# A cross-attention kernel on one core: the scaled gamma and beta made on ScalarE, x's two halves normalised one after the other, and a new table of the order of all calls

## The chip, the cores and the metric

The kernel runs on one core of a Trainium2 chip. The metric is the device time of one execution in microseconds (us), lower is better; a kernel's time is the median of several executions. A core has five engines, each with a queue of its own that it works through in order: TensorE (PE, matmuls; its weight loads are listed as PEld), VectorE (DVE), ScalarE (ACT), GpSimd (POOL) and SyncE (SP, which here only starts DMA transfers). They meet only at semaphores: an instruction at the head of its queue waits until what it reads has been written and what it overwrites has been read. The transfers themselves run on 16 DMA engines that all queues share.

## The reference, cut

```python
# x, ctx: (8, 256, 1024) float32; mask: (8, 256), all true; 32 heads of 32
mu  = mean(x, -1);  var = mean((x - mu)**2, -1)
xn  = (x - mu) * rsqrt(var + 1e-5) * gamma + beta
Q   = split_heads(xn @ Wq.T)                  # (8, 32, 256, 32)
K = V = split_heads(ctx)
scores = einsum('bhsd,bhtd->bhst', Q, K) / sqrt(32)
probs  = softmax(where(mask, scores, -inf), -1)
attn   = einsum('bhst,bhtd->bhsd', probs, V)
out = x + merge_heads(attn) @ Wout.T
```

All matrix products are in float32.

## The kernel before, in words

**Recording and order.** After a few set-up instructions (among them `make_identity`, which writes the 128x128 unit matrix `ident` into the tile `ring` on POOL), the kernel replaces `nc` by `Recorded(nc)` (L356). From there on nothing is issued: each call is only appended to a list, as engine, operation and arguments, and its number is its place in that list, 0 to 6577. The last line of the kernel (L1721) is `nc.issue(ORDER, OTHER)`, which issues the recorded calls in the order of the table `ORDER`, a long string of numbers and ranges (`OTHER` could give a call to another engine and is empty). All calls are issued at one line of that helper, so nearly every row of the profile says L374; the tile names tell them apart. As every engine works through its own queue, only the order of two calls of one engine matters to the time. There is a schedule by hand, so nothing reorders the calls afterwards.

**Work.** Batch b and a group g of four heads make a slot n = 8b+g, 64 in all. In each slot:

- PE makes the scores of the four heads (tile `sc`, eight matmuls of `k` with the projected query `qa`),
- DVE adds the mask and takes the row's extreme (`e`, `mn`), ACT takes the exponential with its row sum (`e<-e,mn`), POOL or ACT scales by the reciprocal sum (`rden`),
- DVE transposes `e` in 32x32 blocks into `pT`; ACT copies half of `pT` aside into `pc`; four DMAs on SP's queue then swap rows between partitions: `pT<-pT` twice, and later `pT<-pc` twice,
- PE forms probabilities times values (`pv`), in many small matmuls from `pT` and `v_all`. `v_all` is one buffer for two slots' values; its next load, on SP's queue, waits until the slots before have read it.

Between these, PE projects the next batch's query (`pq`, and `pq_P` for most batches) from the transposed, normalised input `xnT` and the weights `wq`, and multiplies the results with the output weights `wo` (`po`). Both products are done for pairs of batches in a scheme of seven products instead of eight, which needs sums of blocks of `wq` and `wo` (made on POOL and DVE, some of them kept in device memory by stores on SP's queue: calls 1356 and 1636 are two of those, of half a block sum each). From batch 2 on, `xnT` is also put in place by DMAs on SP (`xnT<-xe`).

**The head.** The change's two lines and most of the prediction stand here. The calls, with their numbers in the list:

- 0 to 31: 32 transposes of `ident` into a tile `busy` that nobody reads. They keep PE running while there is nothing else to do; the table strews them.
- 32, 33: loads of gamma (`gam`) and beta (`bet`), 128x8 each, on ACT's queue. 34 to 37: x of batch 0 (`x`) in four quarters, on SP's queue, as are all of the following: 38, 41 and 43 to 45, 50 to 52 and others, the blocks of `wq` (512 KB each), `k`, the mask and x of the next batches (`load_*`, L466 to L540; issued L558 to L580).
- 55, 56 (L1427, L1428): `gs` = s·gamma and `bs` = s·beta with s = -1/sqrt(32), each 128x8; `bs` is the same tile as `bet`, scaled in place. Before, both are TENSOR_SCALARs on POOL.
- 57 to 60, then 63 to 66 (`ln_stats`, L587): for each half of x_0 (128 of its 256 rows), two BATCH_NORM_STATS on DVE (`st`), their combination (`mv`) and the addition of the epsilon (`ve`); 61 and 67: the power -0.5 on POOL (`rstd`).
- 62 and 86 (`ln_norm`, L612): DVE normalises a half of x in place, 128x1024.
- 68 to 75 (`transpose_x0`, L632): PE transposes the first half's eight 128x128 blocks into `px`; 97 to 104 the second's.
- 76 to 83 (`copy_x0`, L641): the eight blocks go to `xnT` with the scale `gs` and shift `bs`: five on ACT (76, 77, 78, 80, 83: ACTIVATE Identity), three on DVE (79, 81, 82). These are the first ACTIVATEs of the kernel, and ACT's table of functions is loaded ahead of the first of them.
- 84, 85: POOL copies of `bs` into an extra column of `xnT` and of a sum (`h_s1`); both read `bs`.
- 87 to 94 (`first_q`, L650): PE projects the first query block, eight matmuls into `pq`; 95 copies it to `qa`. 105 to 108: scores of slot 0's first half, from `k` and `qa`; then the stream of `pq` matmuls for the second half and the next blocks.

## Time and profile before

| what | value |
|---|---|
| median of 3 runs | 567.06 us (566.14, 570.87, 567.06) |
| the profiled execution's own time | 569.71 us |
| span of the profiled execution | 567.9 us |
| granted TensorE clock over the span | 0.997 |
| instructions | 18645 |
| bytes moved by DMA, mean rate | 113.67 MB, 200 GB/s |

The page gives each engine's busy time and share of the span; then the span in 40 slices of 14.2 us, one digit for the busy tenths of each slice; then the chain of work that ended last, followed back from the last instruction. A row of the timeline reads: start, busy length, engine, line, operation, output<-inputs, partitions x elements and type, how many instructions the row joins, and in square brackets how long the engine had stood idle before it and what released it. In the list of waits, a row names the waiting engine and tile, the work that released it, then total idle time, count and the longest. In the table of stretches, a row has the stretch and its length, then the busy time of PE, PEld, DVE, ACT and POOL with instruction counts, the granted clock, the DMA engines' mean busy share and the GB/s moved. The last rows of the kind "wq<-in_wq_dram SPq ..., 512.0 KB, 9.9" give the median us from the issue of a DMA to its landing. `ring` in a row is the tile that holds the unit matrix at first and sums of blocks later.

### The profile page before, as it was taken

To read this page: it belongs to the slowest core of one execution; us is meant where nothing else is said; L and a number is where in the kernel's file an instruction comes from. 1 tells how busy PE (TensorE), PEld (TensorE's weight loads), DVE (VectorE), ACT (ScalarE), POOL (GpSimd) and SP (SyncE) were. 2 spreads that over 40 slices of the span, in tenths; PEclk is the share of its full clock that TensorE was granted. 3 is DMA by queue.
4 is the path that set the end of the run, shared out by engine and by line. 5 is a ranking of instruction groups with operands and counts; after the bars stand their busy time and mean duration, and the time that the engine had idled before them with its cause. 6 is when DMAs were issued, how large, how long until landed. Compare 5 with 4: busy or idle time off the path is not lost.

```text
span 567.9 us, 18645 instructions
## 1 busy us (share of the span) xinstructions
PE 556.1 (98%) x6570; PEld 371.1 (65%) x6570; DVE 464.3 (82%) x1703; ACT 436.4 (77%) x1461; POOL 410.4 (72%) x621
## 2 busy tenths in 40 slices
PE   6999999998999999999999999999999999999997
PEld 6777776666666766667766676666676577655544
DVE  5899999786988799888878999978767988887724
ACT  2698889785886679878777779879858678979930
POOL 2688989995988976468877955368855777375681
PEclk9999999998999999999999999999999999999999
DMA  8898667687677889797566776778856765674533
GB/s 302 333 268 233 184 173 188 191 238 184 212 222 190 248 216 215 207 265 225 139 191 202 219 203 187 185 215 227 230 136 199 198 169 153 184 220 99 151 94 112
DMA packets 48325, 113.67 MB, mean 200 GB/s; under 512 B 9960, under 2 KB 11624, under 8 KB 48232
## 3 DMA queue, kind: packets, MB, share of 16 engines
q1 hardware_dynamic: 42232, 92.55, 58.4%
q0 software_dynamic: 5712, 19.93, 11.5%
q8 instruction: 52, 0.85, 0.7%
q14 instruction: 41, 0.34, 0.2%
q10 hardware_dynamic: 288, 0.01, 0.0%
HBM read 59.91 MB, written 12.70 MB: 128 GB/s over the span
## 4 chain that ended last, share of the span: by engine, by line
PE 77%; DMA 7%; DVE 7%; ACT 4%; issue 2%; SPq 1%; POOL 1%; DVEq 0%; ACTq 0%
PE pq_P L374 23%; PE po_S L374 17%; PE pv L374 10%; PE sc L374 10%; PE po_A L374 10%; DMA pT<-pT 4%; PE po_end L374 3%; DVE e L374 3%; DVE pT L374 2%; ACT e L374 2%; PE pq L374 2%; DMA pT<-pc 2%; PE ph_P L374 1%; PE po_last L374 1%; SPq L374 1%
## 5 line engine op out<-in xcount | busy, mean ns | idle before, releaser
L374 ACT ACTIVATE e<-e,mn 128x256 f32<-128x256 f32 x512 | 256.1, 502 | 57.8 <-DVE mn L374 45.5
L374 POOL TENSOR_SCALAR e<-e,rden 128x256 f32<-128x256 f32 x368 | 172.2, 480 | 120.6 <-DVE rden L374 118.5
L374 DVE STREAM_TRANSPOSE pT<-e 128x512 f32<-128x512 f32 x256 | 176.7, 700 | 35.9 <-POOL e L374 26.4
L374 DVE CUSTOM_DVE_ANT_0 e<-sc,mb 128x256 f32<-128x256 f32 x512 | 192.6, 410 | 6.0 <-PE sc L374 2.8
L374 PE MATMUL pq_P<-xnT,wq 128*128 128x256 f32 x544 | 132.4, 383 | 0.2 <-DVE qa L374 0.2
L374 PEld LDWEIGHTS pq_P<-xnT,wq 128*128 128x128 f32 x544 | 102.1, 190 | 45.0 <-issue 29.7
L374 ACT ACTIVATION_READ_ACCUMULATOR e<-e,mn 128x1 f32 x512 | 97.0, 190 | 0.0
L374 ACT COPY pc<-pT 128x512 f32<-128x512 f32 x128 | 75.7, 611 | 11.1 <-DMA pT<-pc 6.4
L374 PE MATMUL po_S<-wo,at 128*128 128x512 f32 x152 | 74.5, 601 | 0.0
L374 PE MATMUL pv<-pT,v_all 64*32 64x128 f32 x3584 | 61.5, 277 | 3.0 <-issue 2.1
L374 PEld LDWEIGHTS pv<-pT,v_all 64*32 64x32 f32 x3584 | 53.0, 107 | 14.6 <-issue 9.0
L374 PE MATMUL po_A<-wo,at 128*128 128x512 f32 x128 | 60.9, 602 | 0.0
L374 DVE RECIPROCAL rden<-den 128x2 f32<-128x2 f32 x228 | 32.7, 152 | 29.1 <-ACT e L374 27.8
L374 PE MATMUL po_S<-wo,s 128*128 128x512 f32 x104 | 51.1, 602 | 0.1
L374 PE MATMUL sc<-k,qa 32*128 32x256 f32 x640 | 48.6, 402 | 0.6 <-DMA k<-in_kv_dram 0.5
L374 ACT ACTIVATE e<-e,rden 128x256 f32<-128x256 f32 x88 | 41.5, 502 | 7.0 <-DVE rden L374 6.5
L374 ACT COPY at<-pv 128x128 f32<-128x128 f32 x128 | 30.1, 253 | 17.5 <-PE pv L374 17.5
L374 PEld LDWEIGHTS sc<-k,qa 32*128 32x128 f32 x640 | 30.4, 184 | 19.1 <-issue 8.3
L374 DVE DVE_READ_ACCUMULATOR2_ANT mn<- 128x1 f32 x512 | 42.6, 83 | 0.0
L374 PEld LDWEIGHTS po_S<-wo,at 128*128 128x128 f32 x152 | 27.9, 190 | 19.4 <-issue 15.6
L374 PEld LDWEIGHTS po_A<-wo,at 128*128 128x128 f32 x128 | 23.3, 190 | 22.5 <-issue 19.6
L374 PE MATMUL pq<-xnT,wq 128*128 128x256 f32 (+3 forms) x144 | 31.7, 363 | 1.1 <-ACT xnT L374 0.8
(121 smaller groups left out, 685.8 us busy)
## 6 DMA issues: line engine op xcount, KB each, us to landing
pT<-pT SPq DMA_DIRECT2D x128, 128.0 KB, 3.8
pT<-pc SPq DMA_DIRECT2D x128, 128.0 KB, 4.0
v_all<-in_kv_dram POOLq DMA_DIRECT2D x17, 512.0 KB, 5.7
k<-in_kv_dram SPq DMA_DIRECT2D x30, 256.0 KB, 3.8
r<-in_x_dram SPq DMA_DIRECT2D x26, 256.0 KB, 4.6
xnT<-xe SPq DMA_DIRECT2D x92, 64.0 KB, 3.9
out_dram<-r POOLq DMA_DIRECT2D x18, 256.0 KB, 4.1
wq<-in_wq_dram SPq DMA_DIRECT2D x8, 512.0 KB, 9.9
```

What stands on the lines that cost most here:

```text
L374: getattr(getattr(self.nc, other.get(i, engine)), name)(*a, **k)
```

## The change

The two lines that make `gs` and `bs` become ACTIVATEs with the function Copy on ACT:

```diff
-    nc.gpsimd.tensor_scalar(gs, gam, NEG_SCALE, 1.0, ALU.mult, ALU.mult)
-    nc.gpsimd.tensor_scalar(bs, bs, NEG_SCALE, 1.0, ALU.mult, ALU.mult)
+    nc.scalar.activation(gs, gam, AF.Copy, scale=NEG_SCALE)
+    nc.scalar.activation(bs, bs, AF.Copy, scale=NEG_SCALE)
```

And the whole table `ORDER` is another one. The calls are the same 6578 but for these two; their order is new throughout. Its first rows, and those with the calls that the prediction speaks of (1348 is the load of `v_all` for slots 10 and 11; 1212 and 1213 the `pT<-pc` pair of slot 11; 1356 and 1636 the stores of block sums):

```diff
-32-33 35 34 36-38 43 40 39 42 41 44 51 50 46 45 54-55 0-19 56 58 57 59-60 64 84-85 61-63 65-71 20-24 72-74
-25-26 76-78 80 86-87 75 27 79 82-83 81 88-89 28 97-98 29 90-91 99 92 30 93-95 100-102 31 103-109 111-112 110
-132 123-126 171 170 172 96 114 173 116 119 113 117 115 127-128 133-134 129-131 135 120 137 136 138 121 145-146
...
-1391-1392 1389-1390 1403 1220 1402 1395 1394 1405 1332 1407-1408 1406 1399 1415 1414 1435 1361 1636 1356 1145
-1137-1138 1143 1210 1217 1139 1208 1008 1141 1146 1206 1140 1209 1218 1207 1144 1348 1212 1010 1213 1011
...
+32-33 35 34 36-38 42 40 43 39 41 50 44 47 52 45-46 54 56 55 58 57 59-60 85 0-15 61-62 64 63 65-66 68 16 69-70
+17 71 18-20 72 21-22 73-77 23-25 80-81 78 83-84 67 86-87 26 79 82 88 27-28 89 29-30 97-98 90-95 101 99 31 102
+100 103-112 132 123-126 133 170 96 113 115-117 114 127-130 145-146 171 119-120 131 134 121-122 118 135-136
...
+1009 1139 1008 1214 1212-1213 1010 1148 1219 1314 1348 1362-1369 1373-1378 1297-1298 1379 1299 1380 1300 1387
...
+1435 1573-1580 1445-1508 1513-1516 1429 1555 1354 1581 1636 1422 1356 1421 1631 1353 1641 1544-1546 1434 1520
```

Read by engine, the new head is this. ACT: 56 then 55, then the copies 76, 77, 80, 78, 83. POOL: 85, then 61 (the first `rstd`), then 84 and 67. DVE: the first half's statistics, 62 (its norm), then 64, 63, 65, 66 (the second half's statistics), 81, then 86 (its norm), then 79 and 82; before, 64 stood ahead of 62, and 86 ahead of all three copies. PE: 16 of the `busy` transposes ahead of the first transpose of x (20 before), the others strewn between the next calls. SP: x_0, `wq` block 0, block 1, the mask, x_1's second half, `k`, x_1's first half, then `wq` blocks 5, 2, `k`, 7, 3, 4, x_2, block 6; before: x_0, `wq` block 0, x_1's second half, the mask, `k`, block 1, x_1's first half, blocks 2, 6, 5, 4, 3, x_2, block 7, `k`. Counted per engine, 576 of PE's 3317 calls stand at another place among PE's calls than before, 999 of DVE's 1191, 799 of ACT's 950, 519 of POOL's 612 and 422 of SP's 506. In SP's queue the load of `v_all` 1348 is 139th (136th before), and the stores 1636 and 1356 are 149th and 151st (117th and 118th before).

## The prediction

> **What bounds the kernel now.** I read the page first: the engines' shares, the 40 slices, the chain that ended last.

> ```profile
> span 567.9 us, 18645 instructions
> ...
> PE 556.1 (98%) x6570; PEld 371.1 (65%) x6570; DVE 464.3 (82%) x1703; ACT 436.4 (77%) x1461; POOL 410.4 (72%) x621
> ...
> PE   6999999998999999999999999999999999999997
> ...
> PE 77%; DMA 7%; DVE 7%; ACT 4%; issue 2%; SPq 1%; POOL 1%; DVEq 0%; ACTq 0%
> ```

> TensorE (PE) has matmuls in flight for 556.1 of 567.9 us; all but the first slice is nearly full. The change removes no matmul. So it can gain only where PE waits: at the head, and in a few holes. The list of waits, for PE in the first 20 us, names the head's:

> ```profile
> PE px L374 <- DVE x L374: 1.9, 1, 1.9
> PE busy L374 <- POOL ring masks.py:199: 1.8, 1, 1.8
> PE pq L374 <- ACT xnT L374: 0.8, 1, 0.8
> ```

> The timeline shows this head (start, length, engine, operation; in brackets the idle time before it and what ended it):

> ```profile
> 1.76 4.45 PE L374 MATMUL busy<-ring 128*128 128x128 f32 x20 [1.76 <-POOL ring masks.py:199]
> ...
> 4.43 0.21 POOL L374 TENSOR_SCALAR bet<-bet 128x8 f32<-128x8 f32 x1 [0.52 <-DMA bet<-in_beta_dram]
> ...
> 4.84 0.19 POOL L374 COPY ring<-bet 128x4 f32<-128x4 f32 x1
> ...
> 5.42 0.57 POOL L374 TENSOR_TENSOR rstd<-ve,mhalf 128x1 f32<-128x1 f32 x1 [0.39 <-DVE ve L374]
> ...
> 6.60 0.69 DVE L374 BATCH_NORM_STATS2 st<-x 128x6 f32<-128x512 f32 x1 [1.27 <-DMA x<-in_x_dram]
> 7.21 0.80 DVE L374 TENSOR_SCALAR x<-x,mv,rstd 128x1024 f32<-128x1024 f32 x1
> 7.92 0.69 DVE L374 BATCH_NORM_STATS2 st<-x 128x6 f32<-128x512 f32 x1
> 8.06 0.66 PE L374 MATMUL px<-ring,x 128*128 128x128 f32 x4 [1.86 <-DVE x L374]
> ...
> 8.55 0.71 PE L374 MATMUL busy<-ring 128*128 128x128 f32 x5
> ...
> 8.80 1.28 ACT L374 ACT_TABLE_LOAD   x1 [8.80 <-PE px L374]
> ...
> 9.70 0.81 DVE L374 TENSOR_SCALAR x<-x,mv,rstd 128x1024 f32<-128x1024 f32 x1 [0.67 <-POOL rstd L374]
> 10.10 1.50 ACT L374 ACTIVATE xnT<-px,bet,gs 128x128 f32<-128x128 f32 x4
> ...
> 10.61 0.49 PE L374 MATMUL pq<-xnT,wq 128*128 128x128 f32 x2 [0.80 <-ACT xnT L374]
> ...
> 11.25 0.73 DVE L374 TENSOR_SCALAR xnT<-px,gs,bet 128x128 f32<-128x128 f32 x2 [0.73 <-PE px L374]
> ...
> 12.56 0.41 DVE L374 TENSOR_SCALAR xnT<-px,gs,bet 128x128 f32<-128x128 f32 x1 [0.59 <-ACT xnT L374]
> ...
> 14.66 0.71 PE L374 MATMUL sc<-k,qa 32*128 32x256 f32 x8
> ...
> 15.30 3.79 PE L374 MATMUL pq<-xnT,wq 128*128 128x257 f32 x24
> ```

> Two things here are later than they must be. VectorE (DVE) could normalise the first half of x when rstd ends at 5.42+0.57 = 5.99, but stands before a statistic whose x lands at 6.60, so it starts at 7.21. And ScalarE (ACT) loads its table only when the transposes end at 8.80, 1.28 us on the path. From 15.30 on PE streams.

> **The change, step by step.** POOL loses two tile operations of 0.2 us; ACT gains two ACTIVATEs over 128x8. No row shows that shape. Between the 0.19 us of a 128x4 copy and the 0.27 us of a 128x128 copy I take 0.20, as 8 columns are nearest to 4; the ends differ by 0.14 us over the two. The table load goes ahead of them. In the row above it began when the wait of its ACTIVATE ended, so I let it wait here for beta, which the new table puts first: 4.43. If it does not wait, it is hidden altogether; that end saves another 0.7 us (below).

> First half: load 4.43 to 5.71, bs to 5.91. POOL's queue now has the copy of bs (call 85) **ahead** of the first rstd (call 61): copy 5.95 to 6.14, rstd 6.14 to 6.71. That is 0.72 later than 5.99: a new wait, and behind it stands only what needs rstd. Normalising then runs 6.75 to 7.55 instead of 7.21 to 8.01, and the transposes start at 7.60, 0.46 earlier. The new table puts two filler transposes between the first four, 0.11 each; ACT started 0.74 after them, now 0.74+0.22, at 8.56, and has its table. So the first xnT starts at 8.58 instead of 10.10: **1.52 earlier** (0.46+1.28-0.22).

> Second half: both statistics now follow the norm on DVE, 1.35 us from 7.55 to 8.90. Statistics to norm took 9.70-8.61 = 1.09 before, so the norm runs 9.99 to 10.80, 0.29 **later** than before (9.70 to 10.51). It stays off the path: the last three DVE copies of the first half ended at 12.56+0.41 = 12.97. In the new order one goes before this norm and two (0.73) after it, to 11.55, so 1.42 earlier. The scores stood 1.69 behind that last copy; now 13.24, and the stream starts at 13.88 instead of 15.30. Gain at the head: **1.4 us**.

> Do the loads keep up? Rows by stretch (busy times, then clock, DMA share, GB/s):

> ```profile
> 0.00:3.00 3.00, 1.24 (x6) 1.25 (x7) 0.00 (x0) 0.00 (x0) 1.11 (x8) 1.00 0.29 96
> 3.00:6.00 3.00, 3.00 (x16) 2.88 (x14) 1.75 (x4) 0.00 (x0) 1.30 (x5) 1.00 1.03 337
> 6.00:9.00 3.00, 1.14 (x11) 0.94 (x10) 2.33 (x5) 0.20 (x1) 0.00 (x0) 1.00 0.94 320
> 9.00:12.00 3.00, 2.20 (x20) 1.96 (x19) 1.58 (x4) 2.59 (x5) 0.55 (x1) 1.00 0.97 367
> ```

> By 6.0 us 1.30 MB have moved, by 9.0 2.26, by 12.0 3.36. The four x blocks (1.05 MB) are through at 5.3 and were seen at 6.60, so 1.3 us of notice. wq's first block (1.57 MB) comes at 6.9+1.3 = 8.2, before its first use at 8.58+0.51 = 9.09. k, now behind wq's second block (2.95 MB), comes at 10.9+1.3 = 12.2, 1.0 ahead of the scores. x_1's second half (2.7 MB) comes at 10.2+1.3 = 11.5, when DVE reaches its statistic at 11.55. Of the wq blocks, 2, 4 and 6 stand further back than before; block 6 by most, behind a load that waits for x's buffer:

> ```profile
> 14.76 0.33 SPq L374 DMA_DIRECT2D x<-in_x_dram  x1
> ...
> 25.88 1.28 POOL L374 TENSOR_TENSOR wo<-wq 128x512 f32<-128x512 f32 x1
> ...
> wq<-in_wq_dram SPq DMA_DIRECT2D x8, 512.0 KB, 9.9
> ```

> Issued at 15.09-1.4 = 13.7 it lands by the median of 9.9 at 23.6; POOL's sums read it second now, at 25.88-1.4+1.28 = 25.8. Each of these covers is 0 to 2 us thick; where one is gone, its reader waits as long as the load is late.

> The rest of the table swaps neighbours. Scores stay in runs of eight, values in runs of 32 and 64 head matmuls; what alternates more finely is projection with output products, which costs nothing where operands are there. The holes are where it could matter. The worst, from the chain, the timeline, the DMA view and the stretches:

> ```profile
> 129.65 2.08 issue
> ...
> 122.95 0.53 SPq L374 DMA_DIRECT2D v_all<-in_kv_dram  x1
> ...
> 124.47 0.61 SPq L374 DMA_DIRECT2D xnT<-xe  x1
> ...
> 125.17 0.54 SPq L374 DMA_DIRECT2D pT<-pc  x1
> ...
> v_all<-in_kv_dram SPq DMA_DIRECT2D x1, 512.0 KB, 8.7
> ...
> 132.00:134.00 2.00, 2.00 (x98) 2.00 (x97) 0.41 (x1) 1.58 (x5) 1.81 (x3) 0.57 0.55 150
> 134.00:136.00 2.00, 2.00 (x48) 1.50 (x33) 1.97 (x7) 1.47 (x6) 1.64 (x2) 0.58 0.30 68
> ```

> PE stands from 129.65 to 131.73 for v_all, issued at 122.95 and landed 8.7 us later; then the clock runs at 0.57, which loses 2 x 0.43 + 2 x 0.42 = 1.7 us more. In the new table this load is three places further back in SP's queue (139th, was 136th), 3 x 0.6 = 1.8 us, but two stores of wq halves (1 MB) now stand behind it and not ahead, so it may land faster. Bounds for this place: the hole gone, -3.8; v_all held until the second pT<-pc has gone, +4.7 (below). I take 0, as both effects are of one size.

> Sum: 569.7 us (the profiled execution's own time; 567.9 is its span) less 1.4 is 568.3. That run lies 2.65 above the median of the three runs, 567.06, so against the median 565.66; I say **565.6**, own range 563.5 to 568.

> **Rivals.** (1) *More comes free:* the load waits for nothing (rstd back at 5.42, another 0.7 earlier) or the hole at 129.65 closes. For it: 1 MB of stores no longer stands ahead of v_all. Against it: v_all's own place is later. With the hole gone: 567.06-1.4-3.8 = 561.9.
> (2) *Slower: v_all waits behind a swap.* SP issues in order; the new table has the second pT<-pc of the same pair ahead of v_all, and three xnT moves. If that pT<-pc goes no earlier than 125.17, v_all goes at 125.17+0.54+3 x 0.61 = 127.6, 4.6 later, lands at 136.3, and PE stands 6.7 instead of 2.1 us: 567.06-1.4+4.6 = 570.3. It decides once v_all is issued over 1.4 us later relative to PE.
> (3) *PE starts cold.* The first twenty transposes took 4.45 us, 0.22 each; from 8.06 on a spacing of 0.11. The new table has sixteen before the wait, 3.5 us. If that no longer brings the fast rate, six transposes before ACT's start cost 0.66 more, and eight pq steps up to 1.8: 566.3 to 568.1, say 567.0. [...]

> (4) *ACT is not ready behind its load.* If another 1.28 us stands there (a second table, or something after the load), bs, the first rstd and the norm come that much later, and the gain at the head is 0.1 to 0.2: 566.9. Against it: the load ends at 10.08 and the next ACTIVATE starts at 10.10, and that one load (x1 in the row, and no other in the view by lines) served Identity, Copy and Exp alike. [...]

> **How the numbers follow.** Forecast 0.50, rival (1) 0.18, (2) 0.13, (3) 0.14, (4) 0.05. A step of 1% is 5.7 us, about what a measurement of this kernel tells from no change. Over 1% faster (below 561.4) is about half of rival (1) and a little of unseen holes: 0.12. Over 1% slower (above 572.7) needs a second hole beside rival (2): 0.04. The rest, 0.84, is within 1%. The range takes in most of (1) and (2) whole: 560.5 to 571.

> **What would show it.** Right: ACT's table load starts near 4.4 and ends before the transposes; rstd ends near 6.7; norm near 6.8; first xnT near 8.6; PE's long pq stream starts near 13.9 with wq never its releaser; the hole before pv near 128 is about 2 us. Wrong: a table load at 0 or a second one; PE waiting for wq or k before 25 us; transposes at 0.22 after 7.6; a head gain that is there at 14 and gone by 140, then a hole took it. If the median is below 561 or above 571, not the head but the rest of the table decided, and the step that costed it at 0 failed.

## The result and the profile after

The changed kernel takes 564.01 us (median of 19 runs, 560.58 to 568.27) against 566.87 us before (19 runs, 563.64 to 571.93): ratio 0.9936, 95% interval 0.991 to 0.9962. (A ratio is given here as it was recorded with its interval; it is not the quotient of the two medians, which would be 0.995.) It is faster by about 0.6%, inside the 1% that the prediction took as the bound. The forecast was 565.6, its own range 563.5 to 568. The profiled execution took 564.37 us, against 569.71 before.

The page after, in the lines that the prediction began with (span, engines, the chain that ended last):

```profile
span 562.6 us, 18616 instructions
...
PE 553.0 (98%) x6570; PEld 368.9 (66%) x6570; DVE 467.3 (83%) x1703; ACT 436.3 (78%) x1463; POOL 410.2 (73%) x619
...
PE 90%; DVE 6%; DMA 2%; issue 1%; POOL 1%; ACT 1%; SPq 0%; DVEq 0%; ACTq 0%; POOLq 0%
```

The work is the same; the chain now runs through PE for 90% of the span (77% before), as fewer steps of it hang on transfers (DMA 2%, 7% before). The list of PE's waits, here in part, has at its top one that was not there before, for a sum of blocks of `wo`:

```profile
PE po_S L374 <- POOL wo L374: 1.9, 1, 1.9
...
PE px L374 <- DVE x L374: 1.6, 1, 1.6
PE ph_P L374 <- DVE qa L374: 0.6, 1, 0.6
```

The head, from the timeline (columns as in the prediction):

```profile
1.64 1.28 ACT L374 ACT_TABLE_LOAD   x1 [1.64 <-PEq L1750]
...
4.46 0.21 ACT L374 ACTIVATE bet<-bet 128x8 f32<-128x8 f32 x1 [1.54 <-DMA bet<-in_beta_dram]
...
4.73 0.19 POOL L374 COPY ring<-bet 128x4 f32<-128x4 f32 x1 [3.03 <-ACT bet L374]
...
5.56 0.56 POOL L374 TENSOR_TENSOR rstd<-ve,mhalf 128x1 f32<-128x1 f32 x1 [0.64 <-DVE ve L374]
...
6.15 0.81 DVE L374 TENSOR_SCALAR x<-x,mv,rstd 128x1024 f32<-128x1024 f32 x1 [0.75 <-POOL rstd L374]
...
7.30 0.38 PE L374 MATMUL px<-ring,x 128*128 128x128 f32 x2
...
8.00 1.90 ACT L374 ACTIVATE xnT<-px,bet,gs 128x128 f32<-128x128 f32 x5 [3.23 <-PE px L374]
...
9.33 0.80 DVE L374 TENSOR_SCALAR x<-x,mv,rstd 128x1024 f32<-128x1024 f32 x1
...
10.05 0.72 DVE L374 TENSOR_SCALAR xnT<-px,gs,bet 128x128 f32<-128x128 f32 x2
...
13.23 3.79 PE L374 MATMUL pq<-xnT,wq 128*128 128x257 f32 x24
```

The load of ACT's table waited for nothing; it was over at 2.92. The first xnT copy starts at 8.00 (10.10 before), the long pq stream at 13.23 (15.30 before): 2.07 us earlier.

Where the two profiled executions part can be followed by matching each matmul with the same call's matmul in the profile of before. PE's lead (median over 20 us each) is 2.1 at 20 us, 1.5 at 80, 5.2 at 120, 2.7 at 140, 3.4 at 200, 4.0 at 400 and 5.35 at the end. The lead grows at 130 because before stood still for v_all there (2.08 us), and shrinks at 134 because the changed kernel stands still for a wo sum (1.88 us). Two things had to be explained: whether the head's 2.07 us are there in every execution, and where the new wait comes from.

### The profile page after: what moved, and what is told of

Its sections match the earlier page's. It is cut to its first block, busy times and chain, and to the rows that moved or that the text cites. A ratio compares the mean times of both kernels' runs of the same rounds, so it can differ in the third digit from the quotient of the medians.

```text
span 562.6 us, 18616 instructions
## 1 busy us (share of the span) xinstructions
PE 553.0 (98%) x6570; PEld 368.9 (66%) x6570; DVE 467.3 (83%) x1703; ACT 436.3 (78%) x1463; POOL 410.2 (73%) x619
## 3 DMA queue, kind: packets, MB, share of 16 engines
q0 software_dynamic: 5712, 19.93, 11.5%
## 4 chain that ended last, share of the span: by engine, by line
PE 90%; DVE 6%; DMA 2%; issue 1%; POOL 1%; ACT 1%; SPq 0%; DVEq 0%; ACTq 0%; POOLq 0%
PE pq_P L374 26%; PE po_S L374 19%; PE sc L374 11%; PE pv L374 11%; PE po_A L374 10%; PE pq L374 4%; PE ph_P L374 3%; PE po_end L374 3%; DVE pT L374 2%; DVE e L374 1%; DMA v_all<-in_kv_dram 1%; PE po_last L374 1%; DVE ring L374 1%; PE px L374 1%; DMA x<-in_x_dram 1%
## 5 line engine op out<-in xcount | busy, mean ns | idle before, releaser
L374 ACT ACTIVATE e<-e,mn 128x256 f32<-128x256 f32 x512 | 256.4, 503 | 60.2 <-DVE mn L374 53.1
L374 POOL TENSOR_SCALAR e<-e,rden 128x256 f32<-128x256 f32 x368 | 172.4, 483 | 105.4 <-DVE rden L374 89.9
L374 DVE STREAM_TRANSPOSE pT<-e 128x512 f32<-128x512 f32 x256 | 175.6, 699 | 31.5 <-POOL e L374 20.2
L374 DVE CUSTOM_DVE_ANT_0 e<-sc,mb 128x256 f32<-128x256 f32 x512 | 191.3, 410 | 6.0 <-PE sc L374 3.8
L374 PE MATMUL pq_P<-xnT,wq 128*128 128x256 f32 x544 | 133.2, 382 | 0.0
L374 PEld LDWEIGHTS pq_P<-xnT,wq 128*128 128x128 f32 x544 | 101.9, 190 | 46.9 <-issue 31.5
L374 ACT ACTIVATION_READ_ACCUMULATOR e<-e,mn 128x1 f32 x512 | 97.4, 190 | 0.0
L374 ACT COPY pc<-pT 128x512 f32<-128x512 f32 x128 | 76.7, 612 | 8.3 <-DVE pT L374 6.0
L374 PE MATMUL po_S<-wo,at 128*128 128x512 f32 x152 | 75.3, 600 | 1.9 <-POOL wo L374 1.9
L374 PE MATMUL po_A<-wo,at 128*128 128x512 f32 x128 | 61.1, 601 | 0.0
L374 PE MATMUL pv<-pT,v_all 64*32 64x128 f32 x3584 | 59.1, 272 | 0.3 <-DMA v_all<-in_kv_dram 0.3
L374 PEld LDWEIGHTS pv<-pT,v_all 64*32 64x32 f32 x3584 | 51.3, 105 | 11.3 <-issue 6.4
L374 DVE RECIPROCAL rden<-den 128x2 f32<-128x2 f32 x228 | 33.1, 152 | 27.8 <-ACT e L374 27.2
L374 PE MATMUL po_S<-wo,s 128*128 128x512 f32 x104 | 51.2, 602 | 0.0
L374 ACT ACTIVATE e<-e,rden 128x256 f32<-128x256 f32 x88 | 41.4, 502 | 11.6 <-DVE rden L374 10.8
L374 PE MATMUL sc<-k,qa 32*128 32x256 f32 x640 | 47.9, 401 | 0.0
L374 DVE DVE_READ_ACCUMULATOR2_ANT mn<- 128x1 f32 x512 | 42.3, 83 | 0.0
L374 ACT COPY at<-pv 128x128 f32<-128x128 f32 x128 | 29.8, 256 | 15.4 <-PE pv L374 15.4
L374 PEld LDWEIGHTS sc<-k,qa 32*128 32x128 f32 x640 | 30.0, 184 | 17.6 <-issue 7.2
L374 PEld LDWEIGHTS po_S<-wo,at 128*128 128x128 f32 x152 | 28.0, 190 | 19.5 <-issue 13.9
L374 PEld LDWEIGHTS po_A<-wo,at 128*128 128x128 f32 x128 | 23.4, 190 | 21.8 <-issue 19.5
L374 PE MATMUL pq_P<-xnT,ring 128*128 128x256 f32 x128 | 33.7, 396 | 0.1
## 6 DMA issues: line engine op xcount, KB each, us to landing
v_all<-in_kv_dram POOLq DMA_DIRECT2D x17, 512.0 KB, 6.0
wq<-in_wq_dram SPq DMA_DIRECT2D x8, 512.0 KB, 12.2
```

The lines of the kernel that those rows point to most:

```text
L374: getattr(getattr(self.nc, other.get(i, engine)), name)(*a, **k)
```

## The experiments

All share the runs of the kernel before on their chip (medians 565.92, 566.49 and 566.52 us for the three groups of four). A ratio is to that kernel, with its 95% interval.

**Head alone, rest alone.** The table of the first is the new one up to call 136 and then every other call as in the old table; the second is the old one up to call 146 and then the rest as in the new table, with gs and bs on POOL. The third takes only the two ACT lines, with the old table.

```diff
 # e1: order = new[:to 136] + [c for c in old if not yet there]
 # e2: order = old[:to 146] + [c for c in new if not yet there]; the two lines on gpsimd
 # e3: order = old
-    nc.gpsimd.tensor_scalar(gs, gam, NEG_SCALE, 1.0, ALU.mult, ALU.mult)
+    nc.scalar.activation(gs, gam, AF.Copy, scale=NEG_SCALE)
```

> The new head alone: gs and bs on ScalarE and the first three rows of the new table (up to call 136), then every other call in the order of the old table. Theory A (the gain is the head's, and what stands behind it keeps it): PE's long pq stream starts at 13.2 us as in the changed kernel (15.30 before), the hole at v_all is still there, about 2 us at 127.6 (129.65 less 2.07), and the time is 2.1 us below that of before, ratio 0.996. Theory B (the rest of the table brings most of the gain, and the head's 2.07 us are eaten by waits up to 140 us): the stream starts at 13.2 too, but the time is within 0.8 us of before.

> The old head (gs and bs on GpSimd, the first three rows of the old table, up to call 146), then every other call in the order of the new table. Theory A: the stream starts at 15.3, the wait for v_all near 129 us is gone (its transfer goes ahead of the two stores and lands in under 6 us, 8.7 before), a wait of about 1.9 us of PE for a wo sum stands some 6 us later, and the time is 0.5 to 1 us below that of before, ratio 0.998 to 0.999. Theory B: at least 1.8 us below, ratio 0.997 or less.

> The kernel before with its own table; only the two lines of gs and bs are on ScalarE. Theory A (the table load is 1.28 us of its own, whatever the order): the load starts near 1.6 and waits for nothing, px stays at 8.06, the first xnT copy on ScalarE starts at 8.8 (10.10 before), the pq stream at 14.0 to 14.6 (the second half's norm on DVE, 9.70 to 10.51, may hold some of it back), and the time is 0.7 to 1.3 us below that of before. Rival (the load gives nothing without the new order, as DVE's norm of the second half stands ahead of the first half's last copies): the stream stays within 0.3 us of 15.3.

Measured: e1 565.81 us, 0.9987 (0.996 to 1.0014); e2 564.99 us, 0.9978 (0.9951 to 1.0006); e3 564.99 us, 0.9972 (0.9948 to 0.9996). Neither theory holds in size: each part gives one to three tenths of a per cent, and the intervals of e1 and e2 reach past 1, so neither of these two is told apart from before. The product of head and rest, 0.9965, is just above the interval of the whole change (0.991 to 0.9962); within their own widths the two parts add up to it. The profile of e1 offers a reason why the head gave so little. It is the changed kernel's head, instruction for instruction, but the stream starts at 14.93, not 13.23:

```profile
6.95 0.47 PE L374 MATMUL px<-ring,x 128*128 128x128 f32 x1 [1.51 <-DVE x L374]
7.43 0.64 PE L374 MATMUL px<-ring,x 128*128 128x128 f32 x2
...
8.60 1.51 ACT L374 ACTIVATE xnT<-px,bet,gs 128x128 f32<-128x128 f32 x4 [3.90 <-PE px L374]
```

Two transposes take 0.64 here and 0.38 in the changed kernel's row above. One every 0.215 us, until about 11 us, against one every 0.11. In e3 it is the same:

```profile
1.65 1.28 ACT L374 ACT_TABLE_LOAD   x1 [1.65 <-PEq L1750]
...
7.61 1.12 PE L374 MATMUL px<-ring,x 128*128 128x128 f32 x4 [1.32 <-DVE x L374]
8.83 1.51 ACT L374 ACTIVATE xnT<-px,bet,gs 128x128 f32<-128x128 f32 x4 [4.23 <-PE px L374]
```

Four transposes took 1.12, where the prediction quoted 0.66 from the profile of before. The first xnT copy came 1.47 us ahead of e2's (10.30), as the table load predicts, but the stream started at 15.61 against e2's 15.63: with the slow rate the old head waits for PE's own transposes, and the load is hidden. So both theories had left something out: PE's rate in the head.

**PE's rate.** The same changed kernel once more, and the changed and the old kernel with eight more transposes of the unit matrix ahead of px, so that PE has no long pause (without them it stood from 5.4 us, or from 6.2 or 6.3 in the old order, until x was ready):

```diff
+    for _ in range(8):
+        nc.tensor.transpose(busy, ident, ident)
     nc.issue(ORDER, OTHER)
 # in the table: "85 0-15 61" becomes "85 0-15 6578-6585 61" (e6), "0-19 56" becomes "0-19 6578-6585 56" (e7)
```

> The changed kernel itself, profiled once more. Of the six profiles so far, TensorE transposed the first half of x at 0.11 us each in two (the one of before and the one of the changed kernel) and at 0.215 us in the four others, until about 11 us; the second run of the same new head showed stream starts of 14.9 and 15.0 us and not 13.2. Theory C (the fast rate after 16 transposes is luck of a phase that the kernel does not set): this profile most likely shows the slow rate again, 0.21 per transposition from 7.0 us on, first xnT at 8.6, stream near 15.0. Theory D (the rest of the new table or the chip decided): 0.11 and 13.2 again.

> The changed kernel with eight more transposes of the unit matrix ahead of the first one of x: 24 instead of 16, 24 x 0.215 = 5.2 us from 1.76 to 6.9, so that TensorE has no pause before px. They compute nothing that is read. Theory C: after 5 us without a pause the fast rate comes at the latest some 3.5 us later than it would in the luckiest case, between 5.2 and 8.7 us, in place of about 11: first xnT at 8.0 to 8.6, stream at 13.2 to 14.0, and the time 0.7 to 1.5 us below that of the changed kernel. Theory D: no change of rate or time; the eight transposes even push px back.

> The kernel before with eight more transposes ahead of the first one of x: 28 instead of 20, 1.76 to 7.8 us. Theory C: the rate is fast soon after 7.8 too, but the old head waits for DVE and the table load and not for TensorE: its stream started at 15.30 with the fast rate and at 15.6 with the slow one, so the time changes by 0 to 0.4 us. If it gains 1 us or more, the slow rate cost the old head as much as the new one, and the head's gain in the changed kernel does not depend on it.

The changed kernel again had the slow rate: its median was 563.05 us (8 runs), 0.9936 (0.991 to 0.9961), and its timeline reads

```profile
6.97 0.48 PE L374 MATMUL px<-ring,x 128*128 128x128 f32 x1 [1.54 <-DVE x L374]
...
7.46 0.63 PE L374 MATMUL px<-ring,x 128*128 128x128 f32 x2
...
8.62 1.51 ACT L374 ACTIVATE xnT<-px,bet,gs 128x128 f32<-128x128 f32 x4 [3.92 <-PE px L374]
...
10.22 0.49 PE L374 MATMUL busy<-ring 128*128 128x128 f32 x3
...
14.73 0.70 PE L374 MATMUL pq<-xnT,wq 128*128 128x257 f32 x2
```

Only from 10.22 on do three transposes take 0.49; the stream starts at 14.73. With the eight transposes (e6) PE runs from 1.76 into px, is fast from 7.4 on (5.2 to 8.7 expected), and the stream starts at 13.45:

```profile
1.76 5.38 PE L374 MATMUL busy<-ring 128*128 128x128 f32 x24 [1.76 <-POOL ring masks.py:199]
...
7.52 0.38 PE L374 MATMUL px<-ring,x 128*128 128x128 f32 x2
```

e6 takes 561.6 us, 0.9893 (0.9866 to 0.9921): 1.45 us below the changed kernel beside it, as theory C expected. The old kernel with the eight (e7) takes 564.75 us, 0.9972 (0.9946 to 0.9997): 1.74 us below before by the medians, beyond the 0 to 0.4 us expected, and beyond the 1 us that was named as the sign that the head's gain does not depend on the rate. But its stream starts at 15.60, no earlier, since x was late there (px at 8.35) and not PE. So whatever e7 gained, its profile does not show it at the head.

Over all profiles: with a pause ahead of px the rate was slow in three of five with the new head (streams at 14.73 to 15.00, against 13.23 and 13.28 with the fast rate) and in two of three with the old order of the head (15.6 against 15.30). With eight more transposes the fast rate came in all six, the first fast transposes between 5.8 and 8.5 us.

The kept traces say what the rate is, as each lists the times at which PE's granted clock changed. The first change to the full clock stands at 5.38 us in the first profile of the changed kernel and at 5.52 in e8, but at 10.19 (e5), 10.91 (e1) and 11.05 (e4) with the same head; in the old order at 5.99 (before), 11.11 (e2) and 11.24 (e3); with the eight transposes at 6.71 to 7.88 (e9 lists no change). In all thirteen, transposes came every 0.21 us before that time and every 0.11 after it. All changes that one trace lists lie whole multiples of 3.413 us apart, for example 37 of them from 5.99 to 132.28 in before. Lay these steps back to the start, and the step that ends with the first change is one in which PE was busy for 0.94 or more of the time, while in no earlier step it was busy for more than 0.79. The burst of 16 transposes lasts 3.67 us (1.76 to 5.43), hardly longer than a step. In the first profile of the changed kernel a step lay inside it (1.97 to 5.38); in e1 two steps shared it (0.67 to 4.08 and 4.08 to 7.50, busy for 0.68 and 0.56).

So theory C is shown for the head: with the same 16 transposes the first full clock came at 5.38 in one profile of the changed kernel and at 10.19 in the other, as the steps lay otherwise, and the new head gains about 0.7 us at the stream with the slow rate and 2.07 with the fast one. What the rate is worth at the end is not shown. e6 speaks for 1.45 us; e7 gained as much without an earlier stream, the profiled execution with the slow rate (e5, 562.99 us) is shorter than the one with the fast rate (564.37), and e9 below has the same eight transposes and the ratio of the changed kernel.

**The wait for the wo sum.** In the changed kernel, a sum on DVE that takes 0.66 to 0.75 us in the profile of before took 5.06:

```profile
124.94 2.49 POOL L374 TENSOR_TENSOR xnT<-xnT 128x512 f32<-128x512 f32 x2
...
125.06 5.06 DVE L374 TENSOR_TENSOR ring<-wq 128x512 f32<-128x512 f32 x1
...
127.42 0.93 POOL L374 TENSOR_SCALAR e<-e,rden 128x256 f32<-128x256 f32 x2
...
128.32 1.25 POOL L374 TENSOR_TENSOR wo<-wo 128x512 f32<-128x512 f32 x1
...
130.05 0.15 DVE L374 RECIPROCAL rden<-den 128x2 f32<-128x2 f32 x1
...
130.23 0.91 ACT L374 ACTIVATE e<-e,rden 128x256 f32<-128x256 f32 x2 [3.27 <-DVE rden L374]
...
131.66 0.17 DVE L374 RECIPROCAL rden<-den 128x2 f32<-128x2 f32 x1 [0.88 <-ACT e L374]
...
132.00 0.94 POOL L374 TENSOR_SCALAR e<-e,rden 128x256 f32<-128x256 f32 x2 [2.43 <-DVE rden L374]
...
132.90 1.27 POOL L374 TENSOR_TENSOR wo<-wo 128x512 f32<-128x512 f32 x1
...
134.22 1.25 PE L374 MATMUL po_S<-wo,at 128*128 128x512 f32 x2 [1.88 <-POOL wo L374]
```

POOL ran five instructions without a pause from 124.94 to 129.57, and DVE's sum ended 0.55 us after the last of them. Behind it stood a reciprocal (rden) for which ACT waited 3.27 us. DVE's next reciprocal waited for ACT, and POOL 2.43 us for that one, so that POOL's own next wo sum (132.90) came 1.88 us late for PE. In before another sum on DVE, wo<-wo at 128.15, took 1.51 and also ended 0.55 us after an instruction of POOL that it started beside (127.85 to 129.11). These rows show when the sums ended, and not why. Two runs moved the sum ring<-wq (and wo<-wo, call 1434, behind it):

```diff
-1435 1573-1580 1445-1508 1513-1516 1429 1555 1354 1581 1636 1422 1356 1421 1631 1353 1641 1544-1546 1434 1520
 # e4: "1641 1434" behind 1595
 # e8: 1641 behind 1608, 1434 behind 1614, and
+OTHER = {1434: 'gpsimd'}
```

> The changed kernel with two sums of blocks on DVE (call 1641, ring<-wq, and call 1434, wo<-wo, both with two inputs from SBUF) moved behind call 1595 in the table, some 8 us later in DVE's queue. Theory A (the 5.06 us of ring<-wq at 125 us are a wait for GpSimd's run of five instructions that read SBUF, and that delay makes the wo sum late for PE): DVE goes on with rden and the transposes at 125 to 128 us, PE's wait of 1.9 us for wo near 132 us is gone with the low clock behind it, and the time is 2 to 3.5 us below that of the changed kernel, so 5 to 6 us below before, ratio 0.990. Rival (the sum is long for a reason of its own, its operands or a transfer): it takes about 5 us at its new place too. Rival 2 (another wait takes that hole's place): no gain over the changed kernel, ratio 0.994 to 0.996.

> The changed kernel with the two sums put where they should not meet GpSimd: call 1641 (ring<-wq, DVE) behind call 1608, at a point where GpSimd waits for DVE, and call 1434 (wo<-wo) given to GpSimd behind call 1614. In the last run the moved ring<-wq took 3.48 us again, until 0.5 us after a run of GpSimd instructions ended. [...] Rival: it takes 3 us or more again whatever GpSimd does. Rival 2: it is short, but other waits take its place and the time is that of the changed kernel within 0.8 us.

e4: 566.02 us, 0.9976 (0.9946 to 1.0006), so nothing won over the changed kernel. That is rival 2 at best, as its 0.994 to 0.996 was missed too: the median is 2 us above the changed kernel's. The sum met another run of POOL, took 3.48 us, and made a residual sum late instead:

```profile
131.65 1.28 POOL L374 TENSOR_TENSOR wo<-wo 128x512 f32<-128x512 f32 x1
...
132.14 3.48 DVE L374 TENSOR_TENSOR ring<-wq 128x512 f32<-128x512 f32 x1
132.90 0.94 POOL L374 TENSOR_SCALAR e<-e,rden 128x256 f32<-128x256 f32 x2
...
133.80 1.28 POOL L374 TENSOR_TENSOR xnT<-xnT,xnT 128x512 f32<-128x512 f32 x1
...
138.91 1.12 PE L374 MATMUL po_S<-wo,s 128*128 128x512 f32 x2 [3.13 <-DVE r L374]
```

Again it ended (135.62) 0.54 us after POOL's run (135.08). In e8, at a point where POOL waits for DVE, it took 0.69, as in before, while POOL stood waiting for rden:

```profile
132.61 1.27 POOL L374 TENSOR_TENSOR xnT<-xnT,xnT 128x512 f32<-128x512 f32 x1
...
134.46 0.69 DVE L374 TENSOR_TENSOR ring<-wq 128x512 f32<-128x512 f32 x1
...
135.45 0.93 POOL L374 TENSOR_SCALAR e<-e,rden 128x256 f32<-128x256 f32 x2 [1.57 <-DVE rden L374]
```

What is shown (the expectation of e12 below calls it a lock): the sum is long where it starts within a run of POOL (5.06 and 3.48 us) and short where POOL stands still (0.69). So DVE and POOL meet not only at semaphores, as was said at the start, and where POOL stands matters to DVE though no data passes between these instructions. What in an instruction makes it so, no run shows. That the wait for wo came from it is as good as shown, as it is gone in both runs (which moved the two sums together). That it costs time in the median is not shown: e8 takes 563.3 us, 0.9936 (0.991 to 0.9962), as the changed kernel does, where 1.5 to 3.5 us less was expected. In the second profile of the changed kernel, with the slow rate in the head, the same sum took only 1.26 us and there was no wait for wo (but 1.53 before pv): with the stream 1.5 us later, DVE and POOL meet otherwise there; that this is the reason is argued, not shown.

**Both additions, and the parts undone on top of them.** e9 has the eight transposes and the cleared sums. On this base gs and bs went back to POOL (e10), the statistic went back ahead of the norm (e11), and the second batch's mask was moved (e12):

```diff
 # e10
-    nc.scalar.activation(gs, gam, AF.Copy, scale=NEG_SCALE)
+    nc.gpsimd.tensor_scalar(gs, gam, NEG_SCALE, 1.0, ALU.mult, ALU.mult)
 # e11
-32-33 35 34 36-38 42 40 43 39 41 50 44 47 52 45-46 54 56 55 58 57 59-60 85 0-15 6578-6585 61-62 64 63 65-66 68
+32-33 35 34 36-38 42 40 43 39 41 50 44 47 52 45-46 54 56 55 58 57 59-60 85 0-15 6578-6585 61 64 62-63 65-66 68
 # e12
-748-749 737 750-755 680 762 495-496 368 708 766 769 767 779 902
+748-749 737 750-754 779 755 680 762 495-496 368 708 766 769 767 902
```

> The changed kernel with both additions: eight more transposes ahead of px, and the two sums cleared of GpSimd's run as in the last experiment. With the eight transposes alone the head was fast but PE waited 1.8 us for a wo sum at 132 us; with the sums cleared alone no such wait was there, but whether the head is fast is left to chance. If both are what they seem, here neither cost is there in any execution: stream at 13.2 to 13.8, no wait of PE over 1 us between 15 and 145 us, and a time 1.5 to 3 us below that of the changed kernel (563.1 to 564.0), so 560.3 to 562, ratio 0.985 to 0.990. Rival: with the wo wait gone another wait takes its place further on, and the time is that of the eight transposes alone (561.6).

> The kernel with both additions, but gs and bs are made on GpSimd as before; the order is the same. Theory (the table load costs its 1.28 us wherever it stands behind px): the load starts when ScalarE's wait for px ends, near 8.0, first xnT near 9.4 (8.1 to 8.3 with the lines on ScalarE), the stream 1.2 to 1.3 us later than in the kernel with both additions, and the time 1 to 1.5 us above it. Rival (the load hides beside DVE's copies or the loads of x and wq): stream and time within 0.4 us of that kernel.

> The kernel with both additions, but on DVE the first statistic of x's second half (call 64) again stands ahead of the first half's norm (call 62). Theory (the norm then waits for the landing of x's third quarter, which was there at 6.1 to 6.6 in the old heads): the norm starts at 6.75 to 7.2 in place of 6.1 to 6.2, the stream 0.6 to 1.0 us later, the time 0.5 to 1.1 us above the kernel with both additions. Rival (what PE does next is not bound by the norm of the first half): stream and time within 0.3 us.

> The kernel with both additions, and on DVE the mask of the second batch (call 779, mb<-mk, 128x256 from uint8) moved to directly behind call 754, the last reader of the old mask; there GpSimd has one instruction left before a short pause. In all profiles of the new table so far it took 3.06 to 3.10 us at 71 to 73 us, until just after three GpSimd instructions in a row had ended, against 1.65 in the old table and 0.28 at its shortest; and PE's lead over the kernel before fell by 0.8 to 0.9 us near 80 us. Theory (the same lock as with the sums): mb<-mk takes 0.3 to 1.2 us, PE's wait of 0.6 us for qa near 80 us is gone, and the time is 0.5 to 1 us below the kernel with both additions. Rival: it is short, but the lead is lost near 80 us all the same, and the time is the same within 0.4 us.

e9 takes 562.85 us (6 runs, 561.2 to 564.8), 0.9932 (0.9906 to 0.9957). The profile is what was expected (stream 13.19, no wait of PE over 0.6 us from 15 us on, 561.87 us), the median is not: it misses 0.985 to 0.990, lies 1.25 us above that of e6, and its ratio is that of the changed kernel (0.9936). So the medians do not show that the two additions gain anything together. e10 takes 563.5 us, 0.9943 (0.992 to 0.9965), and its profile shows the load back on the path:

```profile
8.03 1.28 ACT L374 ACT_TABLE_LOAD   x1 [8.03 <-PE px L374]
9.32 1.85 ACT L374 ACTIVATE xnT<-px,bet,gs 128x128 f32<-128x128 f32 x5
```

First xnT 9.32 against 7.96 in e9, stream 14.40 against 13.19: 1.21 us, about the load's length. Part of that is the clock, which became full at 7.32 in e10 and earlier in e9 (fast transposes from 5.83 on); against e6, where it did so at 7.43 and the stream started at 13.45, it is 0.95. Of the 1.21 us some 0.6 are made up by 130 us, and the two profiled executions are 0.54 us apart (562.41 and 561.87). e11 takes 563.2 us, 0.9955 (0.9932 to 0.9978):

```profile
6.86 0.69 DVE L374 BATCH_NORM_STATS2 st<-x 128x6 f32<-128x512 f32 x1 [1.51 <-DMA x<-in_x_dram]
7.47 0.80 DVE L374 TENSOR_SCALAR x<-x,mv,rstd 128x1024 f32<-128x1024 f32 x1
```

The norm at 7.47 against 6.11, the stream at 14.53, 1.34 us later, the execution 0.96 longer (562.83). Here x's third quarter was seen at 6.86, late in the 6.14 to 6.89 of the other profiles in which the statistic waited for it, so 1.34 is near the most that this order costs. Both parts of the head are shown at the stream, at about what their rows say. At the end they are not: 0.54 and 0.96 us are differences of single executions, the medians are 0.65 and 0.35 us above that of e9, and the six runs of e9 alone spread over 3.6 us.

e12 takes 561.53 us (6 runs), 0.991 (0.9886 to 0.9934). In the changed kernel the mask too ended (73.96) just after a run of three instructions of POOL (73.80):

```profile
70.62 1.28 POOL L374 TENSOR_TENSOR ring<-wq 128x512 f32<-128x512 f32 x1
70.88 3.08 DVE L374 TENSOR_SCALAR mb<-mk 128x256 f32<-128x256 uint8 x1
71.84 0.72 POOL L374 TENSOR_TENSOR at<-at,factors 128x256 f32<-128x256 f32 x1
72.53 1.27 POOL L374 TENSOR_TENSOR wo<-wo 128x512 f32<-128x512 f32 x1
```

In e12 it started beside one instruction of POOL (to 70.47) and ended 0.15 us after that:

```profile
68.58 1.89 POOL L374 TENSOR_TENSOR wq<-wq,gs 128x1024 f32<-128x1024 f32 x1
69.94 0.68 DVE L374 TENSOR_SCALAR mb<-mk 128x256 f32<-128x256 uint8 x1
```

PE's wait for qa at 82 us is gone from the list of waits, its lead over the kernel before is 3.05 us at 80 us (1.52 in e9), and the profiled execution takes 560.27 us, the shortest. e12 and e6 have the lowest medians, 1.5 to 2.5 us below the two of the changed kernel (563.05 and 564.01); which of them is the faster their six runs each do not tell. Nor is the move of the mask shown in the median: e12 is 1.32 us below e9, and the two intervals overlap.

## Why the prediction was right, and where it was not

The likeliest case came: a little faster, within 1%. That the gain is the head's, as the sum had it, is shown at the start of the stream and not in the median: the medians lie 2.86 us apart and the sum gave 1.4, the head alone measured 0.9987 and the rest alone 0.9978, neither told apart from 1. The terms of the sum:

- **Table load.** The step "so I let it wait here for beta" was mis-sized, and a load near 0 was one of the prediction's own signs of being wrong. The load began at 1.64 and ended at 2.92; the prediction had 4.43 to 5.71. So bs was ready at 4.67, the copy (call 85) ended at 4.92, and rstd started at 5.56 because ve was ready at 5.40. The new wait of 0.72 on POOL did not exist. The prediction had that end as "another 0.7"; it is about the whole difference (0.65) between its stream at 13.88 and the measured 13.23.
- **Norm of the first half ahead of the statistic.** 6.15, predicted 6.75; with the 0.6 of the step above it is right, and e11 undoes it alone.
- **Second half.** The norm started at 9.33 (predicted 9.99), the last copy of the first half ended at 10.77 (11.55), and neither held PE up. No wq block and no k made PE wait before 25 us.
- **The rate of the transposes.** The working took 0.11 us from one profile. Rival (3), "PE starts cold", came true in three of five profiles of this head, at a price of about 1.5 to 1.8 us at the stream; it had a chance of 0.14 and a price of 0.7 to 2.5 us. The mean stream over these five is 14.23, over the three with the old order 15.51: 1.3 us apart, and 1.4 was forecast. That is luck: the load that waited for nothing and the slow rate, both left out of the sum, cancelled. The same head had the full clock first at 5.38 us in one profile and as late as 11.05 in another; the prediction had the trace of one execution, which shows one such time (5.99) and could not weigh how often it is late.
- **The rest of the table at 0, with the hole at 129.65 kept.** The rest alone measured 0.9978 (0.9951 to 1.0006), so 0 is not refuted, and a gain of some 1 us is as likely. That alternating projection and output products cost nothing in before can be read from its chain: a pq_P matmul took 0.216 us in a row of eight (125.99, 1.73 us) and 0.215 in a row of four between po_S matmuls (137.38, 0.86). The hole of 2.08 us was no fixed part of the table: with the same table behind two other heads it was 1.20 and 0.19 (the rows below). It was read in an execution 2.65 us above the median, and rival (1) took its 3.8 us off the median, where it need not be. How often a hole is that dear, the mean clock of each execution tells: a step of 3.413 us at half clock lowers it to 0.997. Of 74 executions of the kernel before beside the experiments, 32 had 0.997 or less, and took 567.3 us in the mean against 565.8 for the others; of 27 of the changed kernel, five did (565.4 against 563.1). So part of the gain is that such a step came less often. It came in 8 of 36 with the old table behind other heads (e1, e3, e7), so which part of the change does it stays open. In the profile after, the hole is gone, and the wo wait that the prediction did not have took its price back.
- **Rival (4)**: no second load, and nothing behind the one; in e10 the first ACTIVATE starts 0.01 us after it.

The hole before the same 128 pv matmuls, in two more profiles with the old table there, first e1 and then e7: 1.20 and 0.19 us in place of 2.08.

```profile
130.40 2.20 PE L374 MATMUL pv<-pT,v_all 64*32 64x128 f32 x128 [1.20 <-issue]
```

```profile
129.61 2.33 PE L374 MATMUL pv<-pT,v_all 64*32 64x128 f32 x128 [0.19 <-issue]
```

Open: how the gain in the median divides between head and rest, whether the eight transposes and the cleared sums are worth anything there, what e7 gained, and why e10's lateness is partly made up by 130 us.

## What to carry to other kernels

A stream that is bound at the head by an engine with a slow and a fast rate (here 0.21 and 0.11 us for a transpose of PE) must be predicted with both. Here a filler of 24 or 28 transposes brought the fast rate by 8.5 us in all six profiles, where one of 16 or 20 had it before 6 us in three of eight and only from 10.19 us or later in the other five. What happens at the head need not arrive at the end: here 1 to 2 us at the stream were often lost in the spread of the medians. A hole in one profile is first asked for in a second profile, before it is put into a sum. When instructions are reordered on DVE, look in the trace for those that take longer beside a run of POOL, as here the block sums (0.69 to 5.06 us) and the mask's conversion from uint8 (0.68 to 3.08): put them where POOL waits for DVE.
